# A linear-attention and mixture-of-LoRA layer on one core: two groups of projections joined into seven block products, and a bias product moved

## The chip, the cores and the metric

The kernel runs on one core of one Trainium2 chip. The metric is the device time of one execution in microseconds; the time before is the median of three runs. All data is 32-bit float. The names of the engines are those of the profile: PE is the matrix engine and PEld its weight loads, DVE the vector engine, ACT the scalar engine, POOL GpSimd, and SP the engine that issues nearly all DMAs. Each engine works through its instructions in the order in which the program gives them, and waits where an operand or a buffer is not ready yet.

## The reference

Two batches of 1024 tokens with 512 features are normalized. An attention with feature maps and no softmax, and a gated feed-forward layer with low-rank additions (one shared and eight routed, of rank 8 each), both read the normalized tokens and are added to the input.

```python
xn = _layernorm(x)
# attention
Q, K = elu(xn @ wq.T + bq) + 1, elu(xn @ wk.T + bk) + 1          # 16 heads of 32
V = xn @ wv.T + bv
out = (Q @ (K.T @ V)) / (Q @ K.sum(0) + 1e-08)                   # per batch and head
attn = out @ wo.T + bo
# feed-forward, 512 -> 1376 -> 512; w: top-2 of 8 routing weights of each token
gate = xn @ W_gate + lora(xn, sA_gate, sB_gate) + sum_e w_e * lora(xn, A_gate[e], B_gate[e])
up   = xn @ W_up   + lora(xn, sA_up, sB_up)     + sum_e w_e * lora(xn, A_up[e], B_up[e])
hidden = silu(gate) * up
ffn = hidden @ W_down + lora(hidden, sA_down, sB_down) + sum_e w_e * lora(hidden, A_down[e], B_down[e])
return x + attn + ffn
```

## The kernel before

The order of each engine is written out by hand. The two batches are `b` = 0 and 1, and each has two groups `g` of 512 tokens (`TB`). The normalized tokens lie transposed in `xnT[b]`, as four chunks of 128 features. Many products are done by the Winograd form of Strassen's scheme: both operands are cut into 2 x 2 blocks, sums and differences of the blocks are made (`tsum[b]` for the tokens, `wqs` for the query weights), and seven block products take the place of eight. Products 1, 6, 5 and 3 accumulate in one PSUM bank one after the other, and what the bank holds is copied out after each.

The stages, in order of time:

- **Start.** PE transposes an identity 18 times (`WARM`, L249) until the first normalized tokens come. The bias of the keys, `bk`, lands as one row of `bk_sb`; a matmul of that row with a row of ones (`pbk`, L676) spreads it over 128 partitions, and ACT copies it back to `bk_sb` (L677). It stands after the first transposes of tokens (L308). The first key projections (L362) follow.
- **Keys and values**, to about 124 us: key projections (L430), and the sums over tokens of keys times tokens (`pg`, L401).
- **Query unit 0**, to about 165 us: queries of batch 0 (`query_unit`, L772), in which hooks (`P2`, `P1`, `P6`, ...) place the end of the attention's sums. `Finish(1)` takes four banks `pg0` to `pg3` in turn for its products; the four `pko` products are copied to `gt` (L554). Then `shared_factors` (`psa`, L560) takes banks of the next pool, which begins with the same four.
- **Query unit 1 and what goes with it**, to 239.7 us, the part that the change rewrites. The low-rank first factors of gate and up (64 + 64 columns, `agu_sb`) meet the tokens in `low_rank_in(n)` (L851), four matmuls for each batch and group, and are weighted with the routing weights `wT` into `xa[b]`. `denominators(b)` (L873) gives the attention's denominators; those of batch 0 go to DRAM and come back spread over partitions, as eight tiles `bc` in three places, in turn. `attend(0)` multiplies two query tiles at a time by two `bc` tiles (L903), and `spread_den` then issues the four DMAs of the next tile for the place that is free. For batch 1 the spreading is done by matmuls (`pb`, L895). The weights have ten full chunks of 128 columns, done later, and 96 columns are left: `rest(b)` does these for gate and up together, 64 + 64 of them as one part of 128 rows (L1088 with `xa`, L1090 with the tokens) and 32 + 32 as one part of 64 rows (L1077, L1080). `fold_rest(i)` adds the shared low-rank product to the weights of the rest first (L1046, L1049). `gated_rows` ends each part: Silu and a copy on ACT (L1062, L1063), a product on DVE, and a DMA to `r_dram`.
- **The units** (L1202, L1262), to 514.5 us: `unit(j, b)`, ten of them, two levels of the seven-product scheme. `load_weights(j)` loads their weights and `fold_pe`, `fold_adds` and `fold_sums` add the shared low-rank part and make the block sums.
- **The output projection**, to the end.

In the stage of query unit 1 the calls stand like this: `rest_weights`, `low_rank_in(0)`, `denominators(0)`, `low_rank_in(1)`, `token_diffs(0)`, `query_unit(1)` with hooks (two attends each of batch 0 at `P5`, `P7`, `P3`, `P4`, `fold_rest(0)` at `P7`, and `load_weights(0, True)` at `P4`), `load_weights(1)`, `load_last`, `fold_rest(1)`, `low_rank_in(2)`, `low_rank_in(3)`, `denominators(1)`, `rest(0)`, `attend(1)`, `rest(1)`. `hold(v)` is a small clear on DVE of the place that a DMA is to fill, by which the DMA waits for DVE to get there.

Of the kernel before, what the change touches and what calls it, by code (L numbers as in the profile page):

```python
# [15 lines left out]
P = 128  # L16
# [21 lines left out]
def layer_kernel(  # L38
# [55 lines left out]
    WARM = 18  # L94
# [60 lines left out]
    bk_sb = p1.tile([P, D], F32, name="bk_sb")  # L155
    nc.scalar.dma_start(out=bk_sb[0:1, :], in_=bk.unsqueeze(0))
# [91 lines left out]
    for _ in range(WARM):  # L248
        nc.tensor.transpose(warm[:, 0, :], ident, ident)  # L249
# [245 lines left out]
    class Finish:  # L495


        def __init__(self, b, pg, ksum):
            self.b, self.pg, self.ksum = b, pg, ksum
            self.made = 0  # L500
# [166 lines left out]
    for n in range(2):  # L667
        moments(n, 1)
        deviations(n, 1)
        norm(n)  # L670
        load_x(n + 4)
        if n == 0:
            transpose_x(0)

            pbk = bank("pbk", tag="x")
            nc.tensor.matmul(pbk, ones[0:1, :], bk_sb[0:1, :], start=True, stop=True)  # L676
            nc.scalar.copy(bk_sb, pbk)  # L677
# [73 lines left out]
    qt = {}  # L751
# [94 lines left out]
    def low_rank_in(n):  # L846
        b, g = divmod(n, 2)
        cols = ts(g, TB)
        pa = bank(f"pxa{n}")
        for c in range(NC):  # L850
            nc.tensor.matmul(pa, agu_sb[:, c, :], xt(b, c, cols), start=(c == 0), stop=(c == NC - 1))  # L851
        nc.vector.tensor_mul(xa[b][:, cols], pa, wT[b][:, cols])

# [96 lines left out]
    def fold_pe(j, i, tags=()):  # L950

        sb = wsum[j][1]
        pf = []
        for k in range(NC):
            rows = slice(k * 32, k * 32 + RANK)
            name = f"pf{i}_{j}_{k}"
            pf.append(spare_bank(tags[k], name) if tags else bank(name))
            nc.tensor.matmul(pf[k][:, 0 : 2 * P], sat[rows, i, :], sb[rows, i, :, :], start=True, stop=True)
        return pf

    def fold_adds(j, i, pf):
# [3 lines left out]
        for k in range(NC):  # L965
            at = v[:, k // 2 : k // 2 + 7 : 6, k % 2, :]
            nc.vector.tensor_add(at, at, pf[k][:, 0 : 2 * P].rearrange("p (h m) -> p h m", h=2))
# [35 lines left out]
    def token_diffs(b, tag):  # L1003
        xdiff.append(ffn.tile([P, TB], F32, tag=tag, name=f"xdiff{b}"))
        nc.gpsimd.tensor_sub(xdiff[b], xa[b][:, 0:TB], xa[b][:, TB:BT])

    def fold(j, i):
        def f():
            fold_adds(j, i, fold_pe(j, i))
            fold_sums(j, i)  # L1010

        return f
# [10 lines left out]
    def rest_weights():  # L1023
# [5 lines left out]
        bd = both[0 : 2 * ER, (NC + 1) * wide : (NC + 2) * wide]  # L1029
        nc.gpsimd.memset(bd, 0.0)  # L1030
# [7 lines left out]
        return t, sb, bd  # L1038

    def fold_rest(i):  # L1040
        t, sb, _ = w_rest
        pf = []
        for k in range(NC):
            rows = slice(k * 32, k * 32 + RANK)
            pf.append(bank(f"pfr{i}_{k}"))
            nc.tensor.matmul(pf[k][:, 0:REST], sat[rows, i, :], sb[rows, i, :], start=True, stop=True)  # L1046
        for k in range(NC):
            for at, f in zip(rest_cols(i), (slice(0, RA), slice(RA, REST))):
                nc.vector.tensor_add(t[:, k, at], t[:, k, at], pf[k][:, f])  # L1049

    def rest(b, between=(None, None)):
        t, _, bd = w_rest
        spare = [f"qt{k}{g}" for k in range(NC) for g in range(2)]
        blk = [ts(g, TB) for g in range(2)]

        def gated_rows(ps, first, n, g, dst):

            h, v = (
                p2w.tile([P, TB], F32, tag=spare.pop(0), name=f"{n_}{b}_{g}_{dst.start}", bufs=1) for n_ in ("hr", "ur")
            )  # L1060
            gr, ur = slice(first, first + n), slice(first + n, first + 2 * n)
            nc.scalar.activation(h[gr, :], ps[gr, :], AF.Silu)  # L1062
            nc.scalar.copy(v[gr, :], ps[ur, :])  # L1063

            def rest_of():
                nc.vector.tensor_mul(h[gr, :], h[gr, :], v[gr, :])
                nc.sync.dma_start(
                    out=r_dram[b][:, dst, g, :].rearrange("s p n -> p s n"),
                    in_=h[gr, :].rearrange("p (s n) -> p s n", n=UT),
                )  # L1070

            later(rest_of)

        ps = bank(f"pr{b}_2")
        halves = [ps[2 * RB * g : 2 * RB * (g + 1), :] for g in range(2)]
        for g in range(2):
            nc.tensor.matmul(halves[g], bd[:, P:], xa[b][:, blk[g]], start=True, stop=False, skip_group_check=True)  # L1077
        for k in range(NC):
            for g in range(2):
                nc.tensor.matmul(  # L1080
                    halves[g], t[:, k, P:], xt(b, k, blk[g]), start=False, stop=(k == NC - 1), skip_group_check=True
                )
        flush()
        for g in range(2):
            gated_rows(ps, 2 * RB * g, RB, g, slice(RA, REST))
        for g in range(2):
            ps = bank(f"pr{b}_{g}")
            nc.tensor.matmul(ps, bd[:, 0:P], xa[b][:, blk[g]], start=True, stop=False)  # L1088
            for k in range(NC):
                nc.tensor.matmul(ps, t[:, k, 0:P], xt(b, k, blk[g]), start=False, stop=(k == NC - 1))  # L1090
            flush()
# [1075 lines left out]
```

## Time and profile before

| what | us |
|---|---|
| median of 3 runs | 726.39 (724.82 to 728.07) |
| profiled execution | 724.74 |
| its span in the profile | 722.9 |
| PE busy in the span | 714.9 |
| DVE busy in the span | 579.9 |
| start, to 24 us: PE busy | 21.4 |
| query unit 1 and what goes with it, 164.7 to 239.7 us | 75.0, PE busy 75.0 |
| units, 239.7 to 514.5 us | 274.8, PE busy 273.6 |
| output projection, 514.5 us to the end | 208.4, PE busy 205.1 |

The span runs from the first to the last instruction of the profile; the execution's own time has 1.8 us more around it. A line of the timeline reads: start, length, engine, line of the kernel, operation, output and inputs, shapes, and how many instructions are merged; in brackets, how long the engine had been idle and what ended that. A float matmul shows as two records. "idle before" of an engine matters only where the next engine waits for it.

### The profile page before, as it was taken

The numbers are of one execution on the slowest core, as the hardware profiler recorded it, in microseconds if no ns is written. First come the engines' busy times: TensorE is split into PE (matmuls) and PEld (weight loads), VectorE is DVE, ScalarE is ACT, GpSimd is POOL, SyncE is SP. The second block draws the span as 40 slices with busy tenths as digits, with TensorE's granted clock in tenths as the row PEclk, the third lists the DMA queues.
The fourth block names the chain that finished last, engine by engine and source line by source line (L and its number), as shares of the span: only waits on it lengthen the run. The fifth ranks groups of instructions, "written<-read, shape, count | busy, mean of one in ns | idle before, by whom it ended". The sixth has DMA issues, their size and how long they took to land.

```text
span 722.9 us, 9907 instructions
## 1 busy us (share of the span) xinstructions
PE 714.9 (99%) x3428; PEld 491.3 (68%) x3428; DVE 579.9 (80%) x1330; ACT 198.2 (27%) x438; POOL 143.7 (20%) x176
## 2 busy tenths in 40 slices
PE   8999999999999999999999999999999999999998
PEld 6666675454433566567567667566688899899897
DVE  6788766777687688778878878868888889998884
ACT  4434413453442233333333333333200000000000
POOL 4033011101000771311311310544520100000000
PEclk9999999999999999999999999999999999999999
DMA  6343001115585001211201201334653344533101
GB/s 177 99 137 104 0 1 57 42 34 144 131 218 155 19 4 58 88 34 58 88 29 59 88 30 59 117 120 143 204 182 117 117 161 129 158 109 110 59 16 44
DMA packets 61734, 66.85 MB, mean 92 GB/s; under 512 B 10866, under 2 KB 49522, under 8 KB 61428
## 3 DMA queue, kind: packets, MB, share of 16 engines
q1 hardware_dynamic: 61154, 66.20, 29.9%
q8 instruction: 27, 0.44, 0.3%
q14 instruction: 23, 0.19, 0.1%
q10 hardware_dynamic: 530, 0.02, 0.0%
HBM read 44.11 MB, written 22.09 MB: 92 GB/s over the span
## 4 chain that ended last, share of the span: by engine, by line
PE 83%; DVE 13%; ACT 3%; issue 1%; DMA 0%; DVEq 0%
PE ab L1202 16%; PE b L1262 8%; PE po L1942 7%; PE pg L401 5%; PE pya L1771 4%; PE pxa L1771 3%; PE pqu L772 3%; PE pyb L1771 3%; PE ph L1639 3%; PE x L1202 3%; PE pxb L1771 2%; PE pyc L1771 2%; PE pxa L851 2%; PE b L1257 2%; PE pr L1090 2%; PE kua L430 2%
## 5 line engine op out<-in xcount | busy, mean ns | idle before, releaser
L1262 PE MATMUL b<-t,w 128*128 128x512 f32 x160 | 83.2, 601 | 0.8 <-DVE t L1284 0.8
L401 PE MATMUL pg<-kt,xn 128*128 128x512 f32 x128 | 58.7, 594 | 0.5 <-DVE kt L345 0.5
L1284 POOL TENSOR_TENSOR r<-r,r 128x512 f32<-128x512 f32 x20 | 30.1, 1525 | 84.5 <-DVE t L1284 82.9
L1202 PE MATMUL ab<-ti,wi 128*128 128x256 f32 x180 | 45.4, 379 | 0.0
L1202 PEld LDWEIGHTS ab<-ti,w 128*128 128x128 f32 x140 | 25.1, 189 | 29.4 <-DVE r L1230 8.2
L1284 DVE TENSOR_TENSOR r<-r,r 128x512 f32<-128x512 f32 x60 | 44.9, 788 | 0.0
L1202 PEld LDWEIGHTS ab<-ti,wi 128*128 128x128 f32 x180 | 34.2, 190 | 13.2 <-issue 5.0
L1202 PE MATMUL ab<-ti,w 128*128 128x256 f32 x140 | 41.2, 387 | 0.5 <-DVE r L1230 0.2
L401 PEld LDWEIGHTS pg<-kt,xn 128*128 128x128 f32 x128 | 23.2, 190 | 22.6 <-issue 20.6
L1235 ACT COPY r<-ab 128x256 f32<-128x256 f32 x50 | 18.6, 373 | 71.1 <-PE ab L1202 71.1
L1230 DVE TENSOR_TENSOR r<-r,ab 128x256 f32<-128x256 f32 x50 | 20.9, 417 | 20.1 <-ACT r L1227 19.6
L1262 PEld LDWEIGHTS b<-t,w 128*128 128x128 f32 x160 | 29.2, 190 | 11.3 <-issue 5.9
L1238 DVE TENSOR_TENSOR r<-r,ab 128x256 f32<-128x256 f32 x50 | 20.8, 417 | 16.0 <-ACT r L1235 15.7
L1212 ACT COPY r<-ab 128x256 f32<-128x256 f32 x50 | 18.7, 374 | 48.5 <-PE ab L1202 47.1
L1942 PE MATMUL po<-wd,f 128*128 128x256 f32 x140 | 30.9, 380 | 0.1
L410 POOL TENSOR_TENSOR ksum<-ksum,kt 128x512 f32<-128x512 f32 x12 | 15.8, 1318 | 71.7 <-DVE lg L447 42.3
L1223 ACT COPY r<-ab 128x256 f32<-128x256 f32 x50 | 18.6, 373 | 40.8 <-PE ab L1202 40.8
L1942 PEld LDWEIGHTS po<-wd,f 128*128 128x128 f32 x140 | 26.4, 190 | 4.4 <-issue 0.5
L1885 DVE TENSOR_TENSOR f<-f 128x256 f32<-128x256 f32 x84 | 29.3, 417 | 0.1
L1202 PE MATMUL ab<-xnT,w 128*128 128x256 f32 x100 | 29.4, 390 | 0.0
L1202 PE MATMUL ab<-xnT,wi 128*128 128x256 f32 x100 | 28.1, 379 | 0.0
L1202 PEld LDWEIGHTS ab<-xnT,w 128*128 128x128 f32 x100 | 18.1, 189 | 10.8 <-issue 4.5
(482 smaller groups left out, 1652.1 us busy)
## 6 DMA issues: line engine op xcount, KB each, us to landing
h_dram<-h SPq DMA_DIRECT2D x40, 256.0 KB
f<-h_dram SPq DMA_DIRECT2D x10, 512.0 KB
x_ring<-in_x_dram SPq DMA_DIRECT2D x16, 256.0 KB
q_dram<-qt SPq DMA_DIRECT2D x16, 256.0 KB
xr<-in_x_dram SPq DMA_DIRECT2D x16, 256.0 KB
out_dram<-xr SPq DMA_DIRECT2D x15, 256.0 KB
w<-in_w_up_dram SPq DMA_DIRECT2D x10, 256.0 KB
w<-in_w_gate_dram SPq DMA_DIRECT2D x10, 256.0 KB
```

The costliest lines, as they stand in the source:

```text
L401: nc.tensor.matmul(pg[m], xns[n][:, ts(m, P)], kt, start=(j == 0), stop=(j == TPBATCH - 1))
L772: nc.tensor.matmul(banks[c], wqs[p][:, k, ts(c, P)], tsum[b][p][:, k, :], start=(start and k == 0), stop=(k == 1), skip_group_check=True,)
L1202: nc.tensor.matmul(out, w, t, start=start, stop=True, skip_group_check=True)
L1212: nc.scalar.copy(self.r[0][:, H0], self.ua)
L1230: nc.vector.tensor_add(self.r[1][:, H1], self.r[1][:, H1], self.lo)
L1238: nc.vector.tensor_add(self.r[1][:, H0], self.r[1][:, H0], self.lo)
L1262: nc.tensor.matmul(pb[m], ws[m][:, A_OF[p], ts(k, P)], tsum[b][p][:, k, :], start=start, stop=True, skip_group_check=True)
L1284: eng.tensor_add(to[m], t[m], v[m])
L1639: nc.tensor.matmul(phs[u][g * ER : (g + 1) * ER, :], a, f[:, g, :], start=(ns[0] == 0 and n == 0), stop=(last and n == len(chunks) - 1), s ...
L1771: nc.tensor.matmul(o, lhsT, rhs, start=first, stop=True, skip_group_check=True)
L1885: op(t[:, at, :], t[:, x_, :], t[:, y, :])
L1942: nc.tensor.matmul(ps[p][:, q, :], lhsT, rhs, start=start, stop=stop, skip_group_check=True)
```

## The change

The bias product is made with all 128 rows: `bk_sb` is cleared first, the bias lands in its first row, and the matmul takes all rows of ones. It now stands in the warm-up, after 13 of what are now 16 transposes, and its copy ahead of the first tokens' transposes. `Finish` begins with bank `pg3` in place of `pg0`.

`low_rank_in`, `rest` and `fold(j, i)` are gone. The 128 columns of the low-rank factors and the 128 of the rest become the two block rows of one left operand; its block sums are made by `rest_sums` into the spare part of `w_rest`. `low_rank_and_rest` does the seven products for both batches, with hooks for the work that stood between the calls before. `denominators(0)` moves into query unit 1 after its first product; the attends of batch 0 move one hook later each, the last into the new function, as do the loads of the weights of j = 0 and 1, which now follow `load_last`. `fold_rest` does gate and up in one call, and so does the first `fold_pe`.

```diff
-    WARM = 18
+    WARM = 13, 3
...
     bk_sb = p1.tile([P, D], F32, name="bk_sb")
+    nc.vector.memset(bk_sb, 0.0)
     nc.scalar.dma_start(out=bk_sb[0:1, :], in_=bk.unsqueeze(0))
...
+    warm_up(WARM[0])
+
+    pbk = bank("pbk", tag="x")
+    nc.tensor.matmul(pbk, ones, bk_sb, start=True, stop=True)
+    warm_up(WARM[1])
...
-            self.made = 0
+            self.made = NC - 1
...
         if n == 0:
+            nc.scalar.copy(bk_sb, pbk)
             transpose_x(0)
-
-            pbk = bank("pbk", tag="x")
-            nc.tensor.matmul(pbk, ones[0:1, :], bk_sb[0:1, :], start=True, stop=True)
-            nc.scalar.copy(bk_sb, pbk)
...
+        a11, a12 = (agu_sb[:, 2 * k : 2 * k + 2, :] for k in range(2))
+        a21, a22 = (t[:, 2 * k : 2 * k + 2, 0:P] for k in range(2))
+
+        lefts = {1: a11, 2: a12, 3: sums[:, 2], 4: a22, 5: sums[:, 0], 6: sums[:, 1], 7: a21}
...
+    def rest_sums():
+        left = w_rest[3]
+        V = nc.vector
+        V.tensor_add(left[5], left[7], left[4])
+        V.tensor_sub(left[7], left[1], left[7])
+        V.tensor_sub(left[6], left[5], left[1])
+        V.tensor_sub(left[3], left[2], left[6])
+
+    def fold_rest():
...
+        pf = [bank(f"pfr{k}", [P, 2, REST]) for k in range(NC)]
+        for i in range(2):
+            for k in range(NC):
+                rows = slice(k * 32, k * 32 + RANK)
+                nc.tensor.matmul(pf[k][:, i, :], sat[rows, i, :], sb[rows, i, :], start=True, stop=True)
         for k in range(NC):
+            for at, f in ((slice(0, P), slice(0, RA)), (slice(P, None), slice(RA, REST))):
+                v = t[:, k, at].rearrange("p (i n) -> p i n", i=2)
+                nc.vector.tensor_add(v, v, pf[k][:, :, f])
...
+    def low_rank_and_rest(hooks={}):
...
+        def product(p, out, start=False):
+            for b in all_:
+                for k in range(2):
+                    nc.tensor.matmul(
+                        out[b], lefts[p][:, k, :], tsum[b][p][:, k, :], start=(start and k == 0), stop=(k == 1),
+                        skip_group_check=True,
+                    )
...
+        spare = [[place(f"qt{k}{g}", f"g{k}{g}") for k in (b, b + 2) for g in range(2)] for b in all_]
+        c11, u2, u4 = ([place("tmp", f"{n}r0", 3), place(f"bc{i}", f"{n}r1")] for i, n in enumerate(("c11", "u2", "u4")))
...
+        p2_ = banks("pxb")
+        product(2, p2_, True)
+        at("2")
+        up = banks("pxa")
+        product(1, up, True)
+        for b in all_:
+            nc.scalar.copy(c11[b], up[b])
+        for b in all_:
+            V.tensor_add(c11[b], c11[b], p2_[b])
+        for b in all_:
+            V.tensor_mul(xa[b][:, blk[0]], c11[b], wT[b][:, blk[0]])
+        at("1")
+        product(6, up)
+        for b in all_:
+            nc.scalar.copy(u2[b], up[b])
+        at("6")
+        product(5, up)
+        for b in all_:
+            nc.scalar.copy(u4[b], up[b])
+        at("5")
+        product(3, up)
+        for b in all_:
+            V.tensor_mul(xa[b][:, blk[1]], up[b], wT[b][:, blk[1]])
+            token_diffs(b)
+        at("3")
+        low = banks("pr")
+        product(7, low, True)
+        at("7")
+        for b in all_:
+            nc.tensor.matmul(low[b], bd[:, 0:P], xa[b][:, blk[1]], start=False, stop=True, skip_group_check=True)
+        for b in all_:
+            V.tensor_add(u4[b], u4[b], low[b])
+            gated_rows(b, u4[b], 0, RA, 1, slice(0, RA), u4[b], spare[b][0])
...
+        others(0)
+        product(4, low)
+        for b in all_:
+            nc.tensor.matmul(low[b], bd[:, 0:P], xdiff[b], start=False, stop=True, skip_group_check=True)
+        flush()
+        for b in all_:
+            V.tensor_add(u2[b], u2[b], low[b])
+            gated_rows(b, u2[b], 0, RA, 0, slice(0, RA), u2[b], spare[b][3])
+        at("4")
+
+        bank("skip")
+        others(1)
+        flush()
...
     query_unit(1, {
-        "P5": [lambda: attend(0)],
-        "P7": [lambda: fold_rest(0), lambda: attend(0)],
-        "P3": [lambda: attend(0)],
-        "P4": [lambda: attend(0), lambda: load_weights(0, True)],
+        "P2": [lambda: denominators(0)],
+        "P7": [lambda: fold_rest(), lambda: attend(0)],
+        "P3": [lambda: rest_sums(), lambda: attend(0)],
+        "P4": [lambda: attend(0)],
     })
-    load_weights(1)
...
+    low_rank_and_rest({
+        "2": [lambda: attend(0), lambda: load_weights(0, True), lambda: load_weights(1, True)],
+        "6": [lambda: denominators(1)],
+        "5": [lambda: list(token_sums_56(nc.vector, 0, slot(6, [2, 4, TH], "ti56_0")))],
+        "3": [first_fold],
+        "7": [lambda: attend(1, 0), lambda: attend(1, 1)],
+        "64_0": [lambda: fold_sums(0, 0), lambda: fold_sums(0, 1), lambda: token_sums_1(nc.vector, 0)],
+        "4": [lambda: list(inner_weight_sums(nc.vector, 0, (1, 5, 6)))],
+    })
```

`others(b)` is the 64-row part of the rest for one batch: eight matmuls with the tokens, two with `xa`, and two `gated_rows` of 32 + 32 rows. `bank("skip")` takes one bank of the pool and leaves it unused.

## Prediction

> **What bounds the kernel now.** The page first: one engine fills the span.
>
> ```profile
> span 722.9 us, 9907 instructions
> PE 714.9 (99%) x3428; PEld 491.3 (68%) x3428; DVE 579.9 (80%) x1330; ACT 198.2 (27%) x438; POOL 143.7 (20%) x176
> PEclk9999999999999999999999999999999999999999
> ```
>
> PE's share is an average, so next the busy time by windows, cut at the stage that the change touches (columns: window, its length, busy PE, PEld, DVE, ACT, POOL, clock, DMA share, GB/s).
>
> ```profile
> 164.73:175.00 10.27, 10.27 (x43) 4.72 (x44) 6.73 (x8) 3.20 (x9) 1.02 (x5) 1.00 0.59 173
> 175.00:200.00 25.00, 25.00 (x73) 10.87 (x71) 16.60 (x31) 10.24 (x18) 2.10 (x1) 1.00 0.55 133
> 200.00:239.72 39.72, 39.72 (x148) 15.39 (x145) 32.30 (x67) 11.95 (x20) 2.44 (x3) 1.00 0.60 167
> ```
>
> From 164.73 to 239.72 PE is busy without a gap at full clock: a matmul removed here is time gained, and any wait put here is time lost. The other engines' waits are free until PE has to wait for them. The chain of waits (start, length, what) gives PE's prices:
>
> ```profile
> 166.12 3.44 PE pxa L851 x8
> ...
> 200.08 7.06 PE pxa L851 x16
> ...
> 214.84 3.43 PE pr L1090 x8
> ```
>
> A 128x512 f32 matmul is two records, so "x8" is four matmuls: 3.43/4 = 0.86 us each.
>
> **The change part by part.**
>
> *Seven products (gain).* Before, the low-rank input takes 4 calls x 4 matmuls (L851) and the 128-row part of the rest 4 x 4 (L1090): 32. After, 7 products x 2 batches x 2 chunks = 28 of the same shape. 4 x 0.86 = **-3.43 us**. Matmuls with `bd`, the 64-row part, the two folds, the denominators and `pb` keep their number and shape.
>
> *Bank order (`made = NC - 1`).* `psa` waits 0.36 us for ACT L554, the last `gt` copy. The banks now start one later, so `psa0` takes the bank of the first of the four copies, done 1.5 us earlier; `pqx1`, which needs the last copy, comes 1.38 us after `psa0`. **-0.36**, at worst 0.
>
> *The bias product and the start.* The rows from 6.75 us on:
>
> ```profile
> 6.75 1.12 PE L676 MATMUL pbk<-bk_sb,ones 1*128 1x512 f32 x2
> 7.90 0.59 ACT L677 COPY bk_sb<-pbk 128x512 f32<-128x512 f32 x1 [0.66 <-PE pbk L676]
> 8.38 0.21 ACT L268 ACTIVATE sd<-ve 128x1 f32<-128x1 f32 x1
> 8.62 0.16 DVE L277 RECIPROCAL r<-sd 128x1 f32<-128x1 f32 x1 [0.66 <-ACT sd L268]
> ```
>
> After, `pbk` stands inside the warm-up, whose 18 transposes end at 5.47 us while PE waits for `xn` until 6.15: 5 transposes out, one matmul of 0.86 (128 rows) in, 3 transposes left in 16. Its place hides it, and the added clear of `bk_sb` lies on a DVE idle until 3.27. What is gained is not PE's 1.05 us: from 8.6 to 17.2 us DVE has hardly a gap. `ve` was ready at 7.96, but the square root stood behind the copy of `pbk` until 8.38. So DVE's chain gains 0.4; PE's own gain (7.80 to about 6.95, the first `xnT` copy) is 0.85. Bounds 0 and -0.85; I take **-0.5**, nearer to DVE's.
> The Trainium skill ("TensorE: Matmul & The Clock Gate", why this matters for your kernels) says that a matmul with few rows takes the time of a 128-row one; the 1-row record pair here took 1.05 us against 0.86, so the trace disagrees by 0.19. Going by the rule the term stays as it is, since the time is hidden.
>
> *The new wait.* Products 1, 6, 5 and 3 accumulate in one bank for each batch, and ACT must copy the bank before the next product adds to it. PE after the change, from the end of `pqv` at 164.37 and by the chain's lengths: psa 1.38, pqx 3.43, denominators 1.85, three pqu 10.30, pqv 3.43, both rest folds 0.82, pqu and pqv 6.86, products 2 and 1 6.86: it wants product 6 at **199.3**. The copies stand on ACT behind the last exponentials of query unit 1, and these stand behind DVE, which has got more to do in the same hooks. The groups of that spot before:
>
> ```profile
> 195.83 1.28 DVE L784 TENSOR_TENSOR qt<-qt,eq 128x512 f32<-128x512 f32 x2
> 197.03 1.40 DVE L781 TENSOR_SCALAR eq<-pqu,bq_sb 128x512 f32<-128x512 f32 x2
> ...
> 200.76 0.69 DVE L903 TENSOR_TENSOR qt<-qt,bc 128x512 f32<-128x512 f32 x1 [1.73 <-DMA bc<-d_dram]
> ...
> 202.58 1.28 DVE L831 TENSOR_TENSOR qt<-qt,pqv 128x512 f32<-128x512 f32 x2
> 203.77 0.87 DVE L781 TENSOR_SCALAR eq<-qt,bq_sb 128x512 f32<-128x512 f32 x2
> 205.56 0.69 DVE L784 TENSOR_TENSOR qt<-qt,eq 128x512 f32<-128x512 f32 x1 [0.91 <-ACT eq L783]
> 206.69 0.69 DVE L784 TENSOR_TENSOR qt<-qt,eq 128x512 f32<-128x512 f32 x1 [0.44 <-ACT eq L783]
> ```
>
> Product 7 ends at 184.75. DVE then: add 0.7, two `eq` 0.9, the joined rest adds, two attends 1.3, adds 1.3, `eq` 1.4, the four `rest_sums` of 128x256 at 0.42 (row of L971) 1.7, two attends 1.3, adds 1.3 + 1.3, and it starts the last two `eq` at 197.3. The rest adds are eight instead of two times eight, each twice as wide: the old eight took 1.0 us; bounds 0.9 and 2.0, taken 1.5. ACT begins 0.5 later (row 204.28 against 203.77) and needs 2.4 for two Relu and two Exp, so it is free at 200.2, and the first copy (0.59) ends at 200.8: PE waits 1.5. The second copy goes into `bc0`, so it waits until DVE has used the sixth broadcast tile: last adds at 199.1 and 200.2 to 200.9, three attends to 202.8, copy to 203.4; PE, at 202.5 again, waits 0.9. Together 2.4; with the lower price of the rest adds 1.8. I take **+2.1**; bounds 0 (if DVE runs 2 us ahead of my sum) and 4.7 (one stalled SP issue of 2.6, in rival B, on top).
>
> *Behind it.* (a) The eighth broadcast lands about 205 to 206, and `u2r1` is wanted when product 5 reaches batch 1 at 208.7: 2 us of slack. But its multiplication waits at the head of DVE; behind it are the clears that let SP issue the weights of j = 0, then `c11`, the second denominator (3.35 reciprocal), `ti56` and the fold adds. SP issues those weights near 207 instead of 208.5; by the old spacing (first 3.2 us later, then about 1 us each) all four are there by 214 to 216, and DVE adds to them from 217.2. Covered by 1 to 3 us. (b) Eight fold adds end near 220.0; the seventh and eighth `pb` need banks that DVE's attends free at 220.6 and 221.2, PE is there at 220.4: **+0.4**, bounds 0 and 1.0. (c) At the end, unit (0,0) puts its second inner product into the bank of `pr1_2`, which ACT empties with four instructions:
>
> ```profile
> 230.31 0.59 ACT L1062 ACTIVATE hr<-pr 32x512 f32<-32x512 f32 x1 [5.66 <-PE pr L1080]
> 230.92 0.58 ACT L1063 COPY ur<-pr 32x512 f32<-32x512 f32 x1
> 231.52 0.59 ACT L1062 ACTIVATE hr<-pr 32x512 f32<-32x512 f32 x1
> 232.13 0.58 ACT L1063 COPY ur<-pr 32x512 f32<-32x512 f32 x1
> ```
>
> 2.40 us, where PE has 0.43 + 0.43 + 0.86 = 1.72 of other work first: **+0.7**, bounds 0.5 and 0.9. Before, that bank had been empty.
>
> *DVE as a whole.* Six new adds of 0.69 and four of 0.42 (5.8 us), about 1 us saved in the rest adds: 55.6 busy us of 75 become some 60 of 72. Not a bound; it is late only locally.
>
> *Sum.* -3.43 - 0.36 - 0.5 + 2.1 + 0.4 + 0.7 = **-1.1 us**. Against the profiled execution (724.74: 722.9 of span and 1.8 around it) that is 723.6; against the median of the three runs, 726.39, which lies 1.65 above it, 725.3. **I predict 725.3 us.**
>
> **The rivals.** *A, the waits vanish:* if DVE gets through the hooks two microseconds sooner, or the order of ACT is kinder than I read it, all of -4.3 (start at -0.85: -4.6) stays but perhaps 0.5: 721.8 to 722.6. For it: 2 us of stall hang on a sum of a dozen DVE rows, and ACT is only 27% busy. Against: the four-instruction evacuation of (c) and the two copies are simply longer than PE's cover.
>
> *B, the broadcast tiles come late (slower):* place, the sixth and eighth broadcast tiles; each is four DMAs that SP may issue only after DVE has freed the tile three places earlier. Before, these tiles had slack, and DVE still waited 1.73 us at 200.76, after one SP issue took 2.35 us. Their issue-to-landing times in this trace run from 1.86 to 4.22 us. Now PE waits for DVE at just this point. The sixth is issued from 196.4 to 198.2 and wanted at about 202.1: at 1.9 to 2.5 us it is in time, at 4.2 it is 0.3 late, and with one more stalled issue 2.6 late. Every microsecond costs PE one, the weights of j = 0 behind it another once their slack of 1 to 3 us is used. From 1.1 us of lateness on the kernel is slower than before; with two such stalls (4.7) and the weights late by 2, 726.39 - 1.1 + 6 = 731.
> The Trainium skill ("DMA: Bandwidth & Descriptors", anatomy of one DMA) gives about 2.0 us fixed and bytes at 436 GB/s. By it a 64 KB piece needs 2.15 us, rival B never happens and the sum stays; the rows reach twice that under load (DMA share 0.55 to 0.60 here).
>
> *C, not what it says:* fewer matmuls, but of a cost unlike 0.86. The shapes, the clock 1.00 and full row height are the same; I see nothing for it and give it no share.
>
> **How the numbers follow.** Half a per cent, 3.6 us, is about what a measurement of this kernel can tell from no change. Forecast 0.51 (723 to 728), A 0.33, B 0.16. The forecast's own bounds, -4.6 + 0.5 to -1.1 + 2.6 + 0.6 + 0.2 (upper ends of the waits), are 722.3 to 728.7; the range reaches into A: **721.8 to 728.7**. Faster than 722.8 is nearly all of A, 0.33; slower than 730.0 is most of B, 0.15; within, 0.52.
>
> **What would show it.** Two PE waits before product 6 (second line of the seven products) ended by ACT copies of `pxa`, 1.5 and 0.9 us; one before the second `ab` of unit (0,0) ended by ACT, 0.7; none in front of `psa`; the first `pg` some 0.5 earlier; DVE waiting for no `bc` tile longer than 1 us. PE waiting for DMA, or no wait at all, would make the prediction wrong, as would a clock below 1.00 in the first 24 us.

## The result, and the profile after

| | median us | lowest to highest | runs |
|---|---|---|---|
| before | 727.99 | 724.67 to 728.41 | 18 |
| after | 724.35 | 723.78 to 727.01 | 18 |

The medians lie 3.64 us apart. The ratio after/before, which isn't taken from these two medians, is 0.9965, with a 95% interval of 0.9954 to 0.9975: some 2.5 us (1.8 to 3.3) faster, below half a per cent. 725.3 was predicted, from a median of before that was then 726.39.

The two profiled executions tell another story than the medians: 724.74 before, 724.19 after, a difference of only 0.55. The times of before explain that. They lie in three groups: in the 18 runs 2 at 724.7 to 724.8, 5 at 726.2 to 726.4, 11 at 727.9 to 728.4; the profiled execution was one of the lowest group, and the three runs shown at first were one of each. After the change 17 of 18 lie between 723.8 and 725.4. So the change did two things, a small one that traces of nearly equal starts show, and a larger one to the spread.

First the traces. The page after:

```profile
span 722.4 us, 9918 instructions
...
PE 713.5 (99%) x3418; PEld 489.7 (68%) x3418; DVE 586.6 (81%) x1339; ACT 201.9 (28%) x444; POOL 144.4 (20%) x176
```

PE is busy for 1.4 us less than before (714.9), DVE for 6.7 more (579.9), and the span is 0.5 shorter. The windows of the rewritten stage, cut at the first product 1 (195.75), the first `pb` (218.22), the first product of unit (0,0) (237.92) and the end of what is disturbed behind it (columns: window, its length, busy PE, PEld, DVE, ACT, POOL, clock, DMA share, GB/s):

```profile
195.75:218.22 22.47, 21.12 (x73) 8.22 (x71) 18.34 (x40) 6.96 (x11) 1.27 (x1) 1.00 0.79 218
218.22:237.92 19.70, 19.70 (x73) 6.84 (x73) 17.01 (x31) 7.15 (x12) 4.82 (x8) 1.00 0.42 128
237.92:257.00 19.08, 18.03 (x80) 11.73 (x78) 15.74 (x25) 7.35 (x18) 18.77 (x16) 1.00 0.11 24
```

Before, PE had no gap in this stage. Now it has 1.35 us of them from 195.75 to 218.22 and 1.05 behind 237.92. DVE is busy for 17.01 of the 19.70 us from 218.22 to 237.92. PE's waits between 160 and 266 us (who waits, for whom, us in all, how often, the longest):

```profile
PE pxa L1089 <- ACT c11r L1110: 1.4, 2, 0.8
PE ab L1269 <- ACT g L1064: 0.6, 1, 0.6
```

The wait of `psa` (0.4 before) is gone, these two are new, and one at L1329 in unit (0,0) is 0.40, where before it was 0.75. Two losses aren't in this list, as matmuls that wait inside a merged group don't count as idle; PE's timeline shows them by their length (start, length, engine, line, operation, tiles, shapes, count, and in brackets the idle time before):

```profile
218.22 3.62 PE L893 MATMUL pb<-den,spread 32*128 32x512 f32 x16
...
240.56 0.70 PE L1269 MATMUL ab<-t,w 128*128 128x256 f32 x2 [0.65 <-ACT g L1064]
...
245.07 1.25 PE L958 MATMUL pf<-sb,sat 8*128 8x256 f32 x8
```

The sixteen records of `pb` took 2.48 us before and 3.62 now, and the eight of the first fold of j = 1 0.71 before and 1.25 now.

Where each part of the time went, from the start of the same matmul in both traces (the `ab` are counted in records):

| first matmul of | before | after | difference |
|---|---|---|---|
| `pg` (keys times tokens) | 17.18 | 17.08 | -0.10 |
| `psa` | 164.73 | 164.14 | -0.59 |
| unit (0,0), first `ab` | 239.72 | 237.92 | -1.80 |
| unit (0,0), fifth `ab` | 242.31 | 241.53 | -0.78 |
| unit (0,0), 27th `ab` | 253.66 | 253.41 | -0.25 |
| behind it, 53rd `ab` | 263.86 | 263.26 | -0.60 |
| end of the last matmul | 719.74 | 719.20 | -0.54 |

The stage, from `psa` to the first `ab`, gains 1.2 us on PE where 3.4 had been taken out, and unit (0,0) gives back most of what is left. Even the 1.2 are flattered by the trace of before: there the denominators of batch 1 (`pd`, L873) took 2.27 us, and DVE had waited 1.73 us for a broadcast tile. In three traces below whose stage is that of before (only the start of the change; the new place, but one row; the old place, but 128 rows) they took 1.92, DVE waited 1.01 to 1.35, and the stage took 74.64 us in place of 74.99. Against these the stage gains 0.86, which is about 3.43 less the two waits (1.35) and the longer `pb` (1.14), and the end comes only 0.15 to 0.20 earlier once the difference of the first `pg` is taken off.

Why so little is left is shown by the chain of waits between 219 and 262 us (start, length, what):

```profile
219.40 3.56 DVE qt L901 x6
...
224.17 0.69 DVE u4r L1135
...
224.89 0.62 ACT u4r L1063
...
228.15 0.34 DVE w L971
...
234.80 0.70 DVE u2r L1159
...
239.93 0.59 ACT g L1064
...
240.56 0.70 PE ab L1269 x2
```

At 219.4 the chain leaves PE and runs through DVE and ACT for 21 us, to the second product of unit (0,0). Before, the same stretch of the chain was PE alone. PE looks busy in that stretch, but by this chain what it does is no longer what sets the end; an experiment below (`bd` between the two groups of `pb`) tests that.

### The profile page after: what moved, and what is told of

Read it like the earlier page. It is cut to its first block, busy times and chain, and to the rows that moved or that the text cites. A ratio compares the mean times of both kernels' runs of the same rounds, so it can differ in the third digit from the quotient of the medians.

```text
span 722.4 us, 9918 instructions
## 1 busy us (share of the span) xinstructions
PE 713.5 (99%) x3418; PEld 489.7 (68%) x3418; DVE 586.6 (81%) x1339; ACT 201.9 (28%) x444; POOL 144.4 (20%) x176
## 4 chain that ended last, share of the span: by engine, by line
PE 76%; DVE 16%; ACT 2%; issue 2%; DMA 1%; SPq 1%; DVEq 0%; ACTq 0%
PE ab L1269 15%; PE b L1329 8%; PE po L2015 7%; PE pg L410 5%; PE pya L1844 4%; PE pxa L1844 3%; PE pyb L1844 3%; PE ph L1712 3%; PE x L1269 2%; PE pxb L1844 2%; PE pqu L778 2%; PE pyc L1844 2%; PE b L1324 2%; PE kua L439 2%; DVE r L1351 2%
## 5 line engine op out<-in xcount | busy, mean ns | idle before, releaser
L1329 PE MATMUL b<-t,w 128*128 128x512 f32 x160 | 83.2, 601 | 0.4 <-DVE t L1351 0.4
L1329 PEld LDWEIGHTS b<-t,w 128*128 128x128 f32 x160 | 29.2, 190 | 11.0 <-issue 5.9
```

The source lines that it names most:

```text
L1329: nc.tensor.matmul(pb[m], ws[m][:, A_OF[p], ts(k, P)], tsum[b][p][:, k, :], start=start, stop=True, skip_group_check=True)
```

## The experiments

### What the start does: five kernels

**Only the start of the change** (13 + 3 transposes, the full-height bias product between them), in the kernel before.

```diff
-    WARM = 18
+    WARM = 13, 3
...
+    nc.vector.memset(bk_sb, 0.0)
...
+    warm_up(WARM[0])
+    pbk = bank("pbk", tag="x")
+    nc.tensor.matmul(pbk, ones, bk_sb, start=True, stop=True)
+    warm_up(WARM[1])
```

> The kernel before with the start of the changed kernel alone (13 + 3 transposes, full-height bias product between them, cleared bias tile, copy ahead of the transposes). The 18 executions of the kernel before lie in three groups, at about 724.7, 726.3 and 728.1 us, those of the changed kernel nearly all at 724.4. Theory S (the start decides when the PE clock is released, and with it the group): nearly all executions at 724.6 to 725.2, median 724.9, some 3 us below the median of before, although its profile is only 0.1 us better at the first pg than that of the profiled execution before. Theory P (the seven products bring the gain): the three groups stay, median within 0.7 us of that of before.

Measured: median 724.54 (724.07 to 725.75, 9 runs) against 727.96 (32 runs), ratio 0.9963 (0.995 to 0.9975). The upper group is gone: 7 runs lie at 724.1 to 724.9, two at 725.7 and 725.8. The start alone gives what the whole change gives, 3.4 us of the median. How many microseconds of the median that is depends on how many runs of before fall into the upper group: here 18 of 32 did. In the three later series before's median is 726.36 to 726.47, with 12 of 31, 7 of 16 and 4 of 11 in the upper group; from there the same start would be worth some 1.9 us.

PE's first microseconds behind the 13 transposes, in the trace of the whole change:

```profile
4.20 1.98 PE L257 MATMUL pbk<-bk_sb,ones 128*128 128x512 f32 x2
6.01 0.49 PE L252 MATMUL warm<-ident 128*128 128x128 f32 x3
6.56 0.66 PE L317 MATMUL pt<-ident,xn 128*128 128x128 f32 x4
```

The bias product takes 1.98 us, as PE still goes at half pace there (the clock's record begins at 6.0 us), and the first tokens follow with hardly a gap.

**All of the change but the start.**

```diff
-    WARM = 13, 3
+    WARM = 18
...
-    nc.vector.memset(bk_sb, 0.0)
...
-    nc.tensor.matmul(pbk, ones, bk_sb, start=True, stop=True)
...
-            nc.scalar.copy(bk_sb, pbk)
             transpose_x(0)
+            pbk = bank("pbk", tag="x")
+            nc.tensor.matmul(pbk, ones[0:1, :], bk_sb[0:1, :], start=True, stop=True)
+            nc.scalar.copy(bk_sb, pbk)
```

> The changed kernel with the start of before (18 transposes, one-row bias product after the first transposes of tokens). Theory S: three groups again, at about 724.3, 725.9 and 727.7 us, median within 1 us of that of before. Theory P: one group at about 724.4 to 724.9, some 3 us below before.

Measured: median 727.79, ratio 0.9999 (0.9985 to 1.0013), and the three groups are back: 2 runs at 724.92, 3 at 726.3 to 726.5, 7 at 727.8 to 728.1. Theory P has fallen: the seven products and the bank order together give nothing that the medians can tell (the interval is some 1 us either way).

Its profiled execution was one of the upper group. PE's first microseconds, as timeline:

```profile
7.32 2.07 PE L676 MATMUL pbk<-bk_sb,ones 1*128 1x512 f32 x2
9.32 4.82 PE L362 MATMUL pk<-wk_sb,xnT 128*128 128x256 f32 x12
```

Twelve records of `pk` take 4.82 us. In the profiled execution of before, which was in the lowest group, they take 2.90:

```profile
7.80 2.90 PE L362 MATMUL pk<-wk_sb,xnT 128*128 128x256 f32 x12
```

The one-row bias product takes 2.07 against 1.12: PE still runs at half pace, until about 13.3 us, where the clock's record begins and the pace doubles. Before that moment the clock column says nothing: it reads 1.00 while PE gets through six records in 2 us, where before it got through thirteen:

```profile
10.00:12.00 2.00, 2.00 (x6) 1.59 (x5) 1.71 (x6) 0.11 (x2) 2.00 (x3) 1.00 0.17 33
```

**Only the bank order**, in the kernel before.

```diff
-            self.made = 0
+            self.made = NC - 1
```

> The kernel before with the banks of Finish starting at pg3 alone. By the traces: the 0.36 us wait of psa for the last gt copy goes, 0.4 us less in the span of an execution whose first 24 us are alike. Theory S: the groups stay as before (an execution with a mean clock of 0.998 lies 1.6 to 1.8 us above one with 0.999 or 3.4 above one with 1.000), so the median is within 1 us of before. Rival (the wait is taken up by the next product, pqx1): no difference in the span.

Measured: ratio 0.9991 (0.9979 to 1.0003); the groups stay, the middle one at 725.8 to 726.3 (before: 726.2 to 726.8), the upper at 727.5 to 727.9 (727.9 to 728.9). From first `pg` to first `psa` it takes 147.09 us against 147.55: 0.46 gained. At an equal start the end comes 0.29 earlier than in the trace of before. That can't be put down to the bank order, though: the three traces named under the result, which have the old order, lie 0.24 to 0.29 earlier too, since in the trace of before the denominators happened to take 0.35 longer. What the order is worth at the end stays open; by these traces it is 0.3 us at the most.

Its profile caught the middle group. Windows of the start:

```profile
8.00:10.00 2.00, 2.00 (x6) 1.62 (x6) 1.04 (x5) 0.69 (x2) 1.92 (x2) 0.55 0.73 176
10.00:12.00 2.00, 2.00 (x7) 1.56 (x7) 1.93 (x5) 0.20 (x1) 2.00 (x3) 0.59 0.11 25
12.00:24.00 12.00, 11.40 (x50) 8.11 (x49) 9.09 (x28) 5.06 (x13) 2.31 (x4) 1.00 0.23 78
```

The clock had been released, went back to half from about 8.2 to 11.6 us, and came again: one stretch of 3.4 us at half pace, 1.7 us lost. That is the distance between the groups (724.7, 726.4, 728.1), and the mean clocks on record fit it: of the 32 runs of before in this series all 12 of the middle group have 0.998 (one such stretch in 724 us), the two lowest 1.000, and the upper ones 0.995 (two stretches) or 1.000, as a late first release isn't in the record. In this execution PE had idled for 1.13 us before the first tokens and then done the one-row product.

**The new place, but one row.** As the first of these kernels, with the product of one row only, and without the clear of `bk_sb`, which one row doesn't need.

```diff
-    nc.tensor.matmul(pbk, ones, bk_sb, start=True, stop=True)
+    nc.tensor.matmul(pbk, ones[0:1, :], bk_sb[0:1, :], start=True, stop=True)
...
-    nc.vector.memset(bk_sb, 0.0)
```

> The kernel before with the start of the changed kernel, but the bias product still of one row (one row of ones, one row of bias), in the same place between 13 and 3 transposes. If it is the place that counts (PE has no gap before the first tokens' transposes): as the full-height one, one group, median about 724.9. If it is the 128 rows (a product of one row doesn't count as work for the clock): two or three groups remain, median 726 to 728, and in its profile the clock is released later than the 5.7 us of before.

Measured: median 726.9 (723.97 to 727.52), ratio 0.9986 (0.9973 to 0.9999); 2 of 12 runs below 725, where with 128 rows 7 of 9 were and the other two at 725.7 and 725.8. So the place isn't enough; the rows count. The clause on its profile missed: that execution was one of the quick ones, with the clock released at 5.0 us.

**The old place, but 128 rows**, in the kernel before.

```diff
+    nc.vector.memset(bk_sb, 0.0)
...
-            nc.tensor.matmul(pbk, ones[0:1, :], bk_sb[0:1, :], start=True, stop=True)
+            nc.tensor.matmul(pbk, ones, bk_sb, start=True, stop=True)
```

> The kernel before with the bias product of full height (cleared tile, all rows of ones), left at its old place behind the first transposes of tokens. If it is the height that counts as work for the PE clock, wherever it stands: the group at 728 us goes (with the clock released at the end of the stretch that holds the product) and the executions lie at about 724.7 and 726.4, median under 726.6. If it is the place that counts (no gap in PE's work before the first tokens): the three groups stay, median 726.5 to 728.2.

Measured: median 725.68 (724.5 to 726.72), ratio 0.9987 (0.9975 to 1.0), none of 12 runs above 726.8; in before 12 of 31 were. So the height alone takes the upper group away, as expected. Its trace beside that of the bank order points the same way, with one execution each (first the bank order, then this kernel):

```profile
6.33 0.67 PE L308 MATMUL pt<-ident,xn 128*128 128x128 f32 x4 [1.13 <-DVE xn L298]
...
6.55 0.67 PE L309 MATMUL pt<-ident,xn 128*128 128x128 f32 x4 [1.29 <-DVE xn L299]
```

In both the clock was released at 4.8 to 4.9 us, PE then idled, and the bias product followed. With one row and 1.13 us of idling the clock went back to half pace; with 128 rows and 1.29 us it didn't.

About half of the runs are still at 726.1 to 726.7, and its profiled execution (726.10) was one of them, with the clock never lost after its release, so that here this group isn't all clock: PE waits 0.73 us for the router's weights and DVE 2.14 for the second tile of `x`.

```profile
9.25 2.44 PE L363 MATMUL pk<-wk_sb,xnT 128*128 128x264 f32 x10 [0.73 <-DMA wk_sb<-in_w_router_dram]
```

The clear of `bk_sb` holds back ACT's queue: the bias is issued at 1.44 us (0.74 before) and the router's weights behind it at 1.98 (1.29), and they land at 9.11 (4.44). In the changed kernel they land at 7.92, and PE doesn't wait for them. The tile of `x` goes through SP's queue and is issued no later than before (2.12 and 2.13); why it lands at 8.85 (6.84) isn't shown.

### What the seven products give back: seven kernels

All of these change the changed kernel; "at an equal start" means that the difference of the first `pg` is taken off.

**The second c11 copy in another place.**

```diff
-        c11, u2, u4 = ([place("tmp", f"{n}r0", 3), place(f"bc{i}", f"{n}r1")] for i, n in enumerate(("c11", "u2", "u4")))
+        c11 = [place("tmp", "c11r0", 3), spare[1][0]]
+        u2, u4 = ([place("tmp", f"{n}r0", 3), place(f"bc{i}", f"{n}r1")] for i, n in enumerate(("u2", "u4"), 1))
```

> The changed kernel with the second copy after product 1 (c11 of batch 1) put into a spare query tile in place of broadcast tile bc0, so that ACT needn't wait for DVE's third attend. If that copy is what holds product 6 of batch 1: PE's two waits before product 6 go from 0.59 + 0.76 to about 0.6 + 0, and 0.6 to 0.8 us of span at an equal start. Rival (DVE is late as a whole, and the time is given back at the pb products or in unit (0,0)): the first ab no more than 0.3 us earlier.

Measured: median 723.28; at an equal start the first product of unit (0,0) 1.02 earlier and the end 1.00. Of the waits before product 6 only the first is left:

```profile
PE pxa L1089 <- ACT c11r L1111: 0.6, 1, 0.6
```

The second wait hung on the broadcast tile, and nothing took its place.

**`bd` between the two groups of `pb`.**

```diff
-        "7": [lambda: attend(1, 0), lambda: attend(1, 1)],
+        "7": [lambda: attend(1, 0)],
+        "7b": [lambda: attend(1, 1)],
...
             nc.tensor.matmul(low[b], bd[:, 0:P], xa[b][:, blk[1]], start=False, stop=True, skip_group_check=True)
+        at("7b")
```

> The changed kernel with the two matmuls of bd and xa put between the first four and the second four pb products. The eight pb took 3.55 us from the first to the next matmul against 2.48 before. If it is their banks (the seventh and eighth wait for DVE's attends, and then no longer run four at a time): about 1.9 us for two groups of four, PE 0.9 to 1.1 us earlier at the first ab. Rival (DVE's attends set the pace and PE waits for them at the 64-row part instead): no more than 0.3 us.

Measured: the `pb` went as expected, in two groups of 1.14, and the first product of unit (0,0) came 1.4 us earlier at an equal start. And yet the median is 726.08, the end 1.8 later. PE's timeline at the second product of unit (0,0):

```profile
241.74 0.70 PE L1270 MATMUL ab<-t,w 128*128 128x256 f32 x2 [2.65 <-ACT g L1064]
```

The windows of the same kernel, with the clock in the last column but two:

```profile
243.00:246.00 3.00, 3.00 (x8) 2.37 (x8) 2.94 (x3) 0.37 (x1) 3.00 (x3) 0.50 0.31 66
```

What PE gained it had to wait for two products later: 2.65 us in place of 0.65, as DVE's last attends now ended 0.6 later and ACT's emptying came behind them. Behind the wait the clock went to half pace for 3.4 us, which is another 1.7 (some 1.2 of it show at the end, as the fold of j = 1 takes 0.71 there). This is no accident of one execution: 7 of the 10 runs have a mean clock of 0.997 or 0.998. The other three (724.83, 725.02, 725.6) kept the clock and were still no faster than the changed kernel. The rival was right in kind (DVE sets the pace), at another place and at a price that neither theory had named.

**The 64-row part of batch 1 ahead of product 4.**

```diff
         others(0)
+        others(1)
         product(4, low)
...
-        bank("skip")
-        others(1)
...
-        "4": [lambda: list(inner_weight_sums(nc.vector, 0, (1, 5, 6)))],
+        "64_1": [lambda: list(inner_weight_sums(nc.vector, 0, (1, 5, 6)))],
```

> The changed kernel with the 64-row part of batch 1 ahead of product 4, and DVE's inner weight sums ahead of u2. If the four-instruction emptying of pr1_2 by ACT holds the second ab of unit (0,0), and the four gated products that fall together with POOL's sums (6.0 us for four, 1.7 each for the last three, 0.68 elsewhere) hold the fold of j = 1 behind it: the 0.65 wait goes and 0.3 to 0.5 us behind it, 0.7 to 1.2 us of span. Rival (DVE is behind by a fixed amount of work, whatever its order): the wait moves to another matmul and the end stays within 0.3 us.

Measured: median 726.21, the end 1.9 later at an equal start. The wait for `pr1_2` is gone, and in its place PE waits for DVE's sum with `u2`, and then twice for ACT's copies (0.41 and 1.00):

```profile
PE b L1327 <- DVE u2r L1160: 1.3, 1, 1.3
```

The expectation failed and its rival was nearer, though the end was worse than either said.

**Twelve sums from DVE to POOL** (`rest_sums` and the first `fold_sums`).

```diff
-        V = nc.vector
+        V = nc.gpsimd
...
-        "64_0": [lambda: fold_sums(0, 0), lambda: fold_sums(0, 1), ...
+        "64_0": [lambda: fold_sums(0, 0, nc.gpsimd), lambda: fold_sums(0, 1, nc.gpsimd), ...
```

> The changed kernel with the four sums of rest_sums and the eight of the first fold_sums on POOL in place of DVE (5.1 us of DVE work, on an engine that is idle from 171 to 231 us but for 1.3). Theory D (from 219 to 246 us and around 190 to 199 us the order of DVE's work, full without a gap, sets when ACT and then PE go on; the seven products' gain is lost there): the first wait before product 6 (0.59) goes to 0.2 or less, the fold of j = 1 and the fifth L1329 product in unit (0,0) no longer wait (0.54 and 0.35), 0.9 to 1.5 us of span at an equal start. Rival (each of the waits hangs on its own buffer, not on how full DVE is): within 0.3 us, or slower, as POOL and DVE hold each other up.

Measured: median 723.92; 0.49 us of span at an equal start, short of what was expected. One half worked: with `fold_sums` away from DVE the fold of j = 1 takes 0.71 again. The other half gave nothing: the first wait before product 6 was 0.68, and the one at L1329 0.57. DVE's timeline in this kernel, while the four `rest_sums` ran on POOL (187.2 to 191.7):

```profile
188.81 2.34 DVE L790 TENSOR_TENSOR qt<-qt,eq 128x512 f32<-128x512 f32 x2
```

The same two instructions in DVE's timeline of the changed kernel:

```profile
188.81 1.30 DVE L790 TENSOR_TENSOR qt<-qt,eq 128x512 f32<-128x512 f32 x2
```

Two sums before that took 1.82 against 1.29: 1.57 us lost in four, 1.7 saved. And on POOL a `rest_sum` of 128x256 took 1.05 to 1.19 us there, against 0.73 for a `fold_sum` of that size while DVE read from PSUM. Two engines adding tiles of SBUF at once hold each other up. The Trainium skill ("SBUF — State Buffer", Who interferes with whom) states this: a DVE instruction with two inputs in SBUF and a GpSimd instruction that reads SBUF go one after the other, by an exclusive lock. These rows agree.

The same is to be seen in the changed kernel at the end of the stage, where four gated products of DVE meet POOL's token sums (`ti`, 1.60 to 1.71 each; 1.27 in other places). The last two in DVE's timeline:

```profile
241.36 3.43 DVE L1067 TENSOR_TENSOR g<-g,g 32x512 f32<-32x512 f32 x2
```

With the two before them 6.0 us for four, which take 0.68 each elsewhere. That is a part of what made the first fold of j = 1 late by 0.54, but not all: with `fold_sums` on POOL the four take as long (2.61 and 3.42 us), only they begin 1.7 us earlier at an equal start, and the fold isn't late.

**All of these causes away at once**, with one Silu over the 128 rows of the 64-row part as well.

```diff
+            nc.scalar.activation(spare[b][1], ps, AF.Silu)
             for g in range(2):
-                gated_rows(b, ps, 2 * RB * g, RB, g, slice(RA, REST), *spare[b][1:3])
+                gated_rows(b, ps, 2 * RB * g, RB, g, slice(RA, REST), *spare[b][1:3], silu=False)
```

> As the kernel before it, with the other causes taken away too: c11 of batch 1 in a spare query tile, bd matmuls between the two groups of pb products, and the gate and up rows of the 64-row part emptied by one Silu of all 128 rows and two copies (1.8 us in place of 2.4; the up rows that Silu writes are not used). Theory D: no wait before product 6, pb in 1.9 us, 0.1 to 0.2 before the second ab: some 2.5 to 3.5 us of span below the changed kernel at an equal start, median 721.0 to 722.0. Rival (DVE still sets the pace behind pb, as in the run where bd stood between the pb products and PE then waited 2.6 us for ACT): waits before the second ab come back, median above 723.

Measured: median 723.08, 0.92 of span at an equal start: less than the copy alone. The first product of unit (0,0) is 1.4 earlier, and the fold of j = 1 then takes 1.71 for want of DVE. The split of `pb` and `rest_sums` on POOL together did harm, as the next kernel, without these two, shows.

**Those three that help**: c11 in the spare tile, `fold_sums` on POOL, one Silu; against the kernel before it:

```diff
-        V = nc.gpsimd
+        V = nc.vector
...
-        "7": [lambda: attend(1, 0)],
-        "7b": [lambda: attend(1, 1)],
+        "7": [lambda: attend(1, 0), lambda: attend(1, 1)],
```

> The changed kernel with the second c11 copy in a spare query tile, the first fold_sums on POOL, and one Silu over the 128 rows of the 64-row part (rest_sums back on DVE, the pb products in one go). By the runs so far each took away its own wait: 0.76 before product 6, 0.5 at the fold of j = 1, 0.2 at the second ab, 1.3 to 1.7 us of span below the changed kernel at an equal start (first pg at the same time), median 722.4 to 723.0. If DVE's order gives them back, as when bd was put between the pb products: no more than the 0.8 of the copy alone, median 723.3.

Measured: median 721.87 (721.25 to 722.11, 6 runs), ratio to before 0.9934 (0.9914 to 0.9954), and at an equal start 2.81 us of span below the changed kernel, more than expected. The best of all. Its chain of waits over the stretch where the changed kernel's ran through DVE and ACT:

```profile
217.10 3.55 PE pb L893 x16
...
238.74 0.67 PE ab L1272 x2
```

It is PE alone, as in the kernel before. 1.08 of the 2.81 are there at the first product of unit (0,0), by the copy; the rest is the three waits behind it, 0.65 (second product), 0.54 (fold) and 0.40 (L1329), which are all gone. `fold_sums` took the second (0.71 for the fold with it alone). Which edit took the other two isn't shown: with `fold_sums` on POOL and four ACT instructions the first had stayed at 0.62, but the kernel just before had the single Silu too and still waited 0.46 and 0.42 at these places, so taking back the split of `pb` and `rest_sums` has its part.

**No transposes behind the bias product**, on top of that.

```diff
-    WARM = 13, 3
+    WARM = 13, 0
```

> The same with no transposes behind the full-height bias product (13 and 0 in place of 13 and 3). The three end at 6.3 to 6.9 us where the first normalized tokens are there at about 6.15. If they only stand in the way: first transpose of tokens at 6.2, median 0.3 to 0.6 below the kernel before it, all in one group. If the bias product needs them so that PE has no gap: where the clock was released early, PE idles from 5.1 to 6.2, the clock goes back for one window of 3.4 us, and some executions lie 1.5 us and more higher.

Measured: median 722.0 (721.46 to 722.89), the same. The first tokens are transposed at 6.15 and the first `pg` is 0.34 earlier, but `pb` takes 4.31 us in place of 3.62. DVE's timeline has the reason:

```profile
205.12 0.69 DVE L901 TENSOR_TENSOR qt<-qt,bc 128x512 f32<-128x512 f32 x1 [3.63 <-DMA bc<-d_dram]
```

DVE waited 3.63 us for the eighth broadcast tile (2.31 with the three transposes), which came 0.96 later by itself. The gain at the start was lost to a DMA. No execution was 1.5 us higher than the lowest, so the three transposes weren't needed in these 6 runs.

## Why the prediction was right or wrong

**The time** (725.3 for 724.35) came out, the sum behind it only in part, and that the time came out was luck. The sum was -1.1, the two profiled executions show -0.55; without the start it was -0.6, and at an equal start the traces show -0.44 (0.15 to 0.20 against the three traces that have before's stage). The 725.3 stood on a median of three runs with one in each group. From 727.99, the median beside which 724.35 was measured, the same sum gives 726.9. The rest of what the medians show, some 3 us in that series, is the start, which I had at -0.5.

- **The start: the step that failed.** I wrote of the bias product, at 0.86 us, "Its place hides it", with bounds 0 and -0.85 for the whole. In the trace it took 1.98, because PE is still at half pace there; the transposes behind it ended at 6.50, and the first tokens were transposed 0.4 later than before. DVE's chain did gain, as its square root no longer stood behind the copy of `pbk`: the reciprocal behind it came 0.33 earlier (8.29 for 8.62), but by 10.03, where both traces begin the next statistics, nothing of that was left. Net -0.10 in the trace. But in the median the start is worth 3.4, since 16 transposes and a product of 128 rows with hardly a gap let the clock be released in time, and kept it, in nearly every execution, where 18 transposes, an idle stretch of 0.7 to 1.1 us and a product of one row often didn't. The sum was made against one profiled execution, and that was the best kind. The 1.65 us to the median and the spread of three runs (724.82, 726.39, 728.07) stood on the page; I passed them over.
- **Seven products**, -3.43: 28 matmuls of 0.86 as expected.
- **Bank order**, -0.36: -0.46 at `psa`; what of it reaches the end isn't shown, 0.3 at the most.
- **Two waits before product 6**, +2.1: 0.59 + 0.76 = 1.35. The mechanism was right, product 6 was wanted at 199.35 (199.3 predicted), and the first wait was 0.9 shorter mostly because DVE had been overpriced: it started the last two `eq` at 196.5, not 197.3.
- **`pb`**, +0.4: +1.1. The seventh and eighth did wait for banks, but a group of four that is split up by a wait no longer runs four at a time: the seventh and eighth, each behind its bank, took 1.65 us between them, where a whole group of four took 1.14 in another run.
- **Second product of unit (0,0)**, +0.7: 0.65 of idling; by the starts in the table 1.0 is lost up to the fifth record.
- **DVE as a whole**: "Not a bound; it is late only locally" was wrong, though its busy time was forecast well (59.4 us of 73.8 for 60 of 72). From 219.4 us the chain runs through it, so that what PE gained earlier was waited for later (as with the split `pb`), and with 3.4 us of sums taken off DVE the wait of the fold went. The fold of j = 1 (+0.54) wasn't in the sum at all; a shorter wait at L1329 (0.40 for 0.75) was the other way.
- **Rival B**: DVE did wait 2.36 us for the eighth broadcast tile, where I had listed none over 1 us among the signs of being right. In the changed kernel PE lost nothing by it, as DVE waited another 1.51 us for the first `pb` behind it, but it was why the last kernel gained nothing. The fixed 2.0 us and the 436 GB/s that the prediction sets against this rival stand in their section for transfers issued by GpSimd; these tiles are issued by SP, and their own times, 1.86 to 4.22 us in the trace of before, decide. **Rival A** (the waits vanish) is nearly what the best kernel reached by three edits; one wait of 0.58 and the longer `pb` are left in it.

What stays open: which of several causes holds the middle group where the clock isn't lost (the late router weights were seen in one execution only), and why one run of the changed kernel took 727.01: its mean clock of 0.998 tells of one lost stretch, 1.7 us of the 2.7.

## What to carry to other kernels

Look at how the times of a kernel spread before pricing anything against one profile: here the groups at equal distances were states that the start fell into, and a start that keeps PE at work in full-height matmuls until the data comes can be worth more than a better algorithm. Where matmuls are taken out of a stage in which PE has no gap, follow the chain of waits afterwards: if it leaves PE for another engine's queue, the gain is paid out only when that queue is shortened too. Move work to POOL only into stretches in which DVE doesn't add tiles of SBUF.

## What the runs showed of the hardware

- The clock of PE went back to half pace for stretches of 3.4 us: half pace from 8.2 to 11.6 us in one trace, and for 3.4 us behind the 2.65 us wait in another. The Trainium skill ("TensorE: Matmul & The Clock Gate", Part 1) has a free-running window of 3413 ns, which agrees. It puts the way back to half pace behind a whole idle window; here 2.65 us of waiting were enough, or 1.13 us and a one-row product, and the measurement decides. How little work in a stretch is too little wasn't measured.
- For the clock, a matmul of one row isn't the work that one of 128 rows is: at the same place, median 726.9 against 724.54; behind idle stretches of 1.13 and 1.29 us, the clock lost with one row and kept with 128.
- A DVE product of two SBUF tiles took up to 1.75 us in place of 0.68 while POOL added tiles of SBUF, and POOL's sums 1.60 to 1.71 in place of 1.27.
